# Gate products of one batch in seven block products instead of eight, their block sums on VectorE, and a new order of work for the last graph

## The chip, the cores and the metric

The kernel runs on one core of a Trainium2 chip. The core has five engines that run beside each other and wait for each other through semaphores: TensorE (PE, matrix products into the eight banks of PSUM), VectorE (DVE), ScalarE (ACT), GpSimd (POOL) and SyncE (SP, which here only issues DMA). The metric is the device time of one execution in microseconds; lower is better.

## What is computed

64 graphs of 256 nodes with 256 features each pass through two layers. Cut to what matters:

```python
# layer 0, per graph (d = 256)
h = relu(bn1(conv1x1(x)));  h = bn2(conv17(h));  x_conv = relu(h + x)     # conv branch
s = x @ w_se.T + b_se;  A = exp(-dist(s)) * adj
x_nmp = A @ relu(x @ w_msg.T + b_msg)
x_in = concatenate([x_conv, x_nmp])                # 512 features
gi = x_in @ w_ih.T + b_ih                          # 768 columns: r, z, n
gh = x @ w_hh.T + b_hh                             # 768 columns: r, z, n
r = sigmoid(gi_r + gh_r);  z = sigmoid(gi_z + gh_z)
nn = tanh(gi_n + r * gh_n)
x = layernorm(x + (1 - z) * nn + z * x)
# layer 1
h = layernorm(x);  y = relu(adj @ (h @ W_rel) + b_rel + h @ W_root)
out = layernorm(x + y)
```

All of it is float32.

## The kernel before

Everything is written in a fixed order: `manual_schedule` takes each engine's instructions in the order in which the Python code emits them, so the order of calls in the main loop is the order of each queue. PSUM banks come from one pool of eight.

The graphs go in eight batches of eight. The conv branch of a whole batch is one generator, `conv(b)`; it works in the large tile XF (slots V, U, S and S2 of 256 columns each, and HP behind them) with most of its arithmetic on VectorE, and is advanced by `pump()` in small pieces between the steps of the graphs of batch b - 1. While the last batch's graphs run, no batch is left to be convolved, and XF holds nothing that is needed any more.

Graphs are pipelined. In the loop over k (lines 1044 to 1085) one pass does, in this order on PE: the gates of graph k for node half 0 (`gates_rz`, `gates_n`), the transposes of graph k - 1 (`transposes_h`), `gates_rz` for half 1, `passing(k + 1)`, `factors(k + 2)`, `gates_n` for half 1, `project(k - 1)`, `distances(k + 2)`, `messages(k + 3)` and `aggregate(k - 1)`. On VectorE the same pass runs `update(k)` (nn, w, their statistics, h), the evacuation of messages, the mask of k + 2 and the y of k - 1. The last graph, 63, has its own function, `last_graph`, in which each node half is handled by itself.

A gate product has three left operands, each of 256 features by 256 nodes: the transposed x (XT), the message result (NMP) and the conv result (XC). The right operands are w_hh and the two halves of w_ih. For one node half `gates_rz` multiplies six blocks of 128 features by 512 columns (r and z together) into one bank, and `gates_n` does six matmuls of 256 columns into another, since the hidden n part must be kept apart from the input n part:

```python
nc.tensor.matmul(prz, t, wih[:, i, 0:2 * D], start=False, stop=(i == 3))
nc.vector.tensor_add(rz[:, n, :], prz, brzn[:, :2 * D])
nc.scalar.activation(rz[:, n, :], rz[:, n, :], AF.Tanh, scale=0.5)
```

Then `update` (line 733) makes nn from them with two operations of 512 columns on VectorE and a tanh on ScalarE, w with three more, their mean and variance (`stats`), the powers of the variance on GpSimd, and h with two operations that wait for GpSimd. The transposes of the next pass wait for h. `project` copies its two results hr to SBUF on ScalarE, and `aggregate` adds onto the second half of the same banks.

In `last_graph` (line 826) half 0 and half 1 of graph 63 pass through nn, w, h (line 862), `turn_half` (transposes), `project_half` and a last aggregation (line 906), between which the remaining work of graph 62 is placed. Each half of the output is scaled on ScalarE (line 917) with a shift made on GpSimd, and stored by its own DMA.

Of the kernel before, what the change touches and what calls it, by code (L numbers as in the profile page):

```python
# [51 lines left out]
NM = 3 * len(LEAVES) + 2  # L52
SR, ROWS = 32, 36
OB = 7


def tap_matrix():
# [18 lines left out]
def gnn_two_layers(  # L76
# [22 lines left out]
    def bank(name):  # L99
        return psum.tile([P, 512], F32, tag="ps", name=name)  # L100
# [281 lines left out]
    def product(ps, slot, w, m):  # L382
        for c in range(C):
            nc.tensor.matmul(ps, X[:, slot, c * P:(c + 1) * P], w(m, c), start=(c == 0), stop=(c == C - 1))  # L384
# [49 lines left out]
    def conv(b):  # L434
# [122 lines left out]
        def third(j):  # L557
            stt(sl(V + j, 2, 8), sl(V + j, 2, 8), sv[j], sl(U + j, 2, 8))
            yield cost(2)
# [25 lines left out]
            yield from second(j)  # L585
        for j in range(8):
            yield from third(j)

        def channels(q):
            for o in range(C):  # L590
# [26 lines left out]
    def load(k):  # L617

        if k >= B:
            return  # L620
        load_xt(k)
        load_adj(k)
# [9 lines left out]
    def load_x(k):  # L632
        if k < B:
            XG[k] = work.tile([P, C, D], F32, tag="x", name="x")
            nc.sync.dma_start(out=XG[k], in_=x[k].rearrange("(c p) d -> p c d", p=P))
# [83 lines left out]
    def gates_n(k, n):  # L719
# [5 lines left out]
            nc.tensor.matmul(pn[:, :D], t, wih[:, i, 2 * D:], start=(i == 0), stop=(i == 3))  # L725
        nc.vector.tensor_add(RZ[k][1][:, n, :], pn, brzn[:, 2 * D:])  # L726

    def stats(mv, k, src):
        st = work.tile([P, 6], F32, tag="bst", name="bst", bufs=4)
        nc.vector.bn_stats(st, src)  # L730
        nc.vector.bn_aggr(mv[:, k, :], st)  # L731
# [49 lines left out]
    def project(k):  # L781
        hT = H[k]
        hr = work.tile([P, C, D], F32, tag="hr", name="hr", bufs=1)
        outs = []
        for n in range(C):
            ps = bank("ps_out")
            for c in range(C):
                nc.tensor.matmul(ps, hT[:, c, n * P:(n + 1) * P], wrr[:, c, :], start=(c == 0), stop=(c == C - 1))  # L788
            nc.scalar.copy(hr[:, n, :], ps[:, :D])
            outs.append(ps)  # L790
        OUTS[k] = (hr, outs)
# [29 lines left out]
    def step(g):  # L821
        if g is not None:
            next(g, None)


    def last_graph(y_before, k):
        nn, w, y = (work.tile([P, C, D], F32, tag=t, name=t, bufs=b) for t, b in (("nn", 1), ("w", 1), ("y", 2)))
        H[k] = work.tile([P, C, D], F32, tag="h", name="h", bufs=1)
        X1[k] = work.tile([P, C, D], F32, tag="x1", name="x1", bufs=2)

        hT, hr = (XF[:, i * C * D:(i + 1) * C * D].rearrange("p (c n) -> p c n", c=C) for i in range(2))
        outs = []

        def scales(mv, columns):

            q = work.tile([P, 2], F32, tag="q", name="qh", bufs=4)
            for i, (f, e) in enumerate(columns):
                nc.gpsimd.tensor_scalar(q[:, i:i + 1], mv[:, 1:2], f, e, ALU.mult, ALU.add)
            nc.gpsimd.tensor_tensor(q[:, :len(columns)], q[:, :len(columns)], mhalf[:, :len(columns)], ALU.pow)
            return q  # L840

        def shift(mv, q):
            sh = work.tile([P, 1], F32, tag="sh", name="shh", bufs=4)
            nc.gpsimd.tensor_mul(sh, mv[:, 0:1], q[:, 0:1])
            nc.gpsimd.tensor_scalar(sh, sh, -1.0, None, ALU.mult)
            return sh

        def half(n):
            rz, gn = RZ[k]
            a, c = nn[:, n, :], w[:, n, :]  # L850
            stt(a, rz[:, n, :D], 1.0, gn[:, n, D:], op0=ALU.add, op1=ALU.mult)
            stt(a, a, 0.5, gn[:, n, :D])
            nc.scalar.activation(a, a, AF.Tanh)
            yield
            nc.vector.tensor_sub(c, XG[k][:, n, :], a)
            stt(c, rz[:, n, D:], 3.0, c, op0=ALU.add, op1=ALU.mult)
            stt(c, a, 4.0, c)
            mv = work.tile([P, 1, 2], F32, tag="mv", name="mvh", bufs=4)
            stats(mv, 0, c)
            mv = mv[:, 0, :]  # L860
            q = scales(mv, [(1.0, 4 * EPS), (1 + EPS, 4 * EPS * EPS)])
            nc.vector.tensor_scalar(H[k][:, n, :], c, mv[:, 0:1], q[:, 1:2], ALU.subtract, ALU.mult)
            sh = shift(mv, q)
            yield
            nc.scalar.activation(X1[k][:, n, :], c, AF.Identity, bias=sh, scale=q[:, 0:1])
            yield

        def turn_half(n):
            ps = bank("ps_hT")
            for c in range(C):  # L870
                nc.tensor.transpose(ps[:, c * P:(c + 1) * P], H[k][:, n, c * P:(c + 1) * P], ident)
            for c in range(C):
                nc.scalar.activation(hT[:, c, n * P:(n + 1) * P], ps[:, c * P:(c + 1) * P], AF.Identity,
                                     bias=gb[:, 1, c:c + 1], scale=gb[:, 0, c:c + 1])

        def project_half(n):
            ps = bank("ps_out")
            for c in range(C):
                nc.tensor.matmul(ps, hT[:, c, n * P:(n + 1) * P], wrr[:, c, :], start=(c == 0), stop=(c == C - 1))
            nc.scalar.copy(hr[:, n, :], ps[:, :D])  # L880
            outs.append(ps)

        halves_ = [half(n) for n in range(C)]
        gates_rz(k, 0)
        gates_n(k, 0)
        step(y_before)
        transposes_h(k - 1)
        step(halves_[0])
        gates_rz(k, 1)
        step(halves_[0])  # L890
        step(halves_[0])
        gates_n(k, 1)
        step(halves_[1])
        turn_half(0)
        project(k - 1)
        project_half(0)
        step(halves_[1])
        turn_half(1)
        agg = aggregate(k - 1)
        step(agg)  # L900
        project_half(1)
        step(halves_[1])
        step(agg)
        for m in range(C):
            for n in range(C):
                nc.tensor.matmul(outs[n][:, D:], ADJ[k][:, m, n * P:(n + 1) * P], hr[:, m, :], start=False,
                                 stop=(m == C - 1), skip_group_check=True)
        step(agg)
        for n in range(C):
            o = y[:, n, :]  # L910
            nc.vector.tensor_add(o, outs[n][:, D:], brel)
            stt(o, o, 0.0, X1[k][:, n, :], op0=ALU.max, op1=ALU.add)
            mv = work.tile([P, 1, 2], F32, tag="mv3", name="mvy", bufs=4)
            stats(mv, 0, o)
            q = scales(mv[:, 0, :], [(1.0, EPS / 4)])
            sh = shift(mv[:, 0, :], q)
            nc.scalar.activation(o, o, AF.Identity, bias=sh, scale=q[:, 0:1])
            (nc.sync, nc.scalar)[n].dma_start(out=out[k, n * P:(n + 1) * P, :], in_=o)


# [107 lines left out]

    POINTS = 10
    y_left = None  # L1030
    for b in range(NB):
        coming = conv(b + 1) if b + 1 < NB else iter(())
        done, at, goal = 0.0, 0, BG * POINTS - 6

        def pump():
            nonlocal done, at
            at += 1
            while done < CONV_WEIGHT * at / goal:
                t = next(coming, 1e9)
                if t is None:  # L1040
                    break
                done += t

        for k in range(b * BG, min((b + 1) * BG, B - 1)):
            load(k + 3)
            load_x(k + 1)
            up = update(k)
            agg = None
            gates_rz(k, 0)
            pump()  # L1050
            gates_n(k, 0)
            step(y_left)
            pump()
            if k > 0:
                transposes_h(k - 1)
            pump()
            gates_rz(k, 1)
            pump()
            if k + 1 < B:
                passing(k + 1)  # L1060
            pump()
            if k + 2 < B:
                factors(k + 2)
            gates_n(k, 1)
            pump()
            if k > 0:
                project(k - 1)
            step(up)
            pump()
            if k + 2 < B:  # L1070
                distances(k + 2)
            step(up)
            pump()
            if k + 3 < B:
                messages(k + 3)
            step(up)
            pump()
            if k + 2 < B:
                mask(k + 2)
            if k > 0:  # L1080
                agg = aggregate(k - 1)
            step(agg)
            step(agg)
            pump()
            y_left = agg
        for _ in coming:
            pass
    last_graph(y_left, B - 1)


# [41 lines left out]
```

## Time and profile before

| | us |
|---|---|
| median of 8 runs | 2267.99 |
| lowest, highest | 2265.56, 2270.48 |
| the profiled execution | 2267.9 |
| its span in the profile | 2266.1 |
| a graph of the last batch, gate to gate | 25.60 |
| from the last graph's first gate to the end | 37.6 |

The costliest groups of the gates, from the page (line, engine, operation, output from inputs, shapes, count, then busy time in us and mean ns of one, then the engine's idle time before them):

```profile
L711 PE MATMUL ps_rz<-whh,xT 128*128 128x512 f32 x512 | 240.8, 593 | 0.0
L713 PE MATMUL ps_rz<-wih,nmp 128*128 128x512 f32 x512 | 240.6, 592 | 0.0
L713 PE MATMUL ps_rz<-wih,xc 128*128 128x512 f32 x512 | 240.6, 592 | 0.0
L716 DVE TENSOR_TENSOR rz<-ps_rz,brzn 128x512 f32<-128x512 f32 x128 | 87.0, 680 | 189.5 <-PE ps_rz L713 189.5
...
L723 PE MATMUL ps_n<-whh,xT 128*128 128x256 f32 x512 | 131.6, 379 | 0.0
L725 PE MATMUL ps_n<-wih,xc 128*128 128x256 f32 x512 | 131.4, 379 | 0.0
L725 PE MATMUL ps_n<-wih,nmp 128*128 128x256 f32 x512 | 131.4, 379 | 0.0
```

A matmul of the program has two records. Durations of neighbouring records overlap, so the pace of a row of matmuls is read from the starts.

### The profile page before, as it was taken

What the parts mean: (1) busy time and instruction counts of PE and PEld (TensorE: products, weight loads), DVE (VectorE), ACT (ScalarE), POOL (GpSimd) and SP (SyncE); (2) the same over time, 40 slices, a digit from 0 to 9 for tenths busy, and PEclk for the clock granted to TensorE, in tenths of its full rate; (3) what the DMA queues carried; (4) which work ended last, traced back from release to release, by engine and by line L of the source; (5) the groups of instructions that cost most, each with busy time, mean ns of one, the idle gap of its engine ahead of it and who ended that gap; (6) DMA issues with size and microseconds to landing.
All of it is one profiled execution on the core that took longest, in us unless ns stands there. A gap on an engine that the chain in (4) does not pass through costs nothing.

```text
span 2266.1 us, 24485 instructions
## 1 busy us (share of the span) xinstructions
PE 2219.3 (98%) x8386; PEld 1459.2 (64%) x8386; DVE 1678.3 (74%) x3194; ACT 767.9 (34%) x1588; POOL 470.5 (21%) x935
## 2 busy tenths in 40 slices
PE   8999999999999999999999999999999999999998
PEld 5775666666665666656666566666666666666664
DVE  6976889388882988749886597946889388884444
ACT  6433223432234322443224422243222532233333
POOL 0101212221220221213122121221222122221122
PEclk9999999999999999999999999999999999999999
DMA  5932432314423153232522243231433214421100
GB/s 146 313 105 71 139 107 93 101 44 139 135 75 103 38 170 100 79 103 80 162 80 83 85 130 121 74 112 52 139 106 99 93 48 133 140 75 38 43 28 19
DMA packets 212682, 226.68 MB, mean 100 GB/s; under 512 B 22104, under 2 KB 203855, under 8 KB 212559
## 3 DMA queue, kind: packets, MB, share of 16 engines
q1 hardware_dynamic: 190128, 191.27, 26.7%
q10 hardware_dynamic: 22430, 33.86, 4.3%
q8 instruction: 67, 1.10, 0.2%
q14 instruction: 57, 0.46, 0.1%
HBM read 179.22 MB, written 45.88 MB: 99 GB/s over the span
## 4 chain that ended last, share of the span: by engine, by line
PE 80%; DVE 14%; DMA 2%; issue 2%; POOL 1%; ACT 1%; SPq 0%; ACTq 0%; POOLq 0%; DVEq 0%
PE ps_rz L713 17%; PE ps_k L384 10%; PE ps_rz L711 8%; PE ps_n L725 8%; PE ps_out L788 7%; PE ps_c L465 5%; PE ps_nmp L695 5%; DVE XF L103 4%; PE ps_n L723 4%; PE ps_out L800 4%; PE ps_msg L645 4%; PE ps_w L229 2%; DMA w<-w2m 2%; DVE w L103 1%; DVE bst L730 1%
## 5 line engine op out<-in xcount | busy, mean ns | idle before, releaser
L103 DVE SCALAR_TENSOR_TENSOR XF<-XF 128x512 f32<-128x512 f32 (+2 forms) x800 | 507.4, 664 | 7.4
L752 POOL TENSOR_SCALAR q<-mv 128x2 f32<-128x2 f32 x63 | 31.8, 505 | 1453.1 <-DVE mv L731 1453.1
L384 PE MATMUL ps_k<-w,XF 128*128 128x256 f32 x1316 | 298.3, 382 | 14.6 <-ACT AT L685 11.6
L384 PEld LDWEIGHTS ps_k<-w,XF 128*128 128x128 f32 x1316 | 246.5, 190 | 61.1 <-ACT AT L685 17.2
L726 DVE TENSOR_TENSOR gn<-ps_n,brzn 128x512 f32<-128x512 f32 x128 | 87.9, 687 | 236.7 <-PE ps_n L725 236.7
L717 ACT ACTIVATE rz<-rz 128x512 f32<-128x512 f32 x128 | 80.6, 630 | 509.1 <-DVE rz L716 509.1
L711 PE MATMUL ps_rz<-whh,xT 128*128 128x512 f32 x512 | 240.8, 593 | 0.0
L713 PE MATMUL ps_rz<-wih,nmp 128*128 128x512 f32 x512 | 240.6, 592 | 0.0
L713 PE MATMUL ps_rz<-wih,xc 128*128 128x512 f32 x512 | 240.6, 592 | 0.0
L716 DVE TENSOR_TENSOR rz<-ps_rz,brzn 128x512 f32<-128x512 f32 x128 | 87.0, 680 | 189.5 <-PE ps_rz L713 189.5
L788 PE MATMUL ps_out<-wrr,hT 128*128 128x512 f32 x504 | 226.6, 592 | 0.0
L713 PEld LDWEIGHTS ps_rz<-wih,xc 128*128 128x128 f32 x512 | 97.3, 190 | 122.5 <-issue 122.2
L713 PEld LDWEIGHTS ps_rz<-wih,nmp 128*128 128x128 f32 x512 | 97.3, 190 | 122.5 <-issue 122.5
L788 PEld LDWEIGHTS ps_out<-wrr,hT 128*128 128x128 f32 x504 | 95.7, 190 | 96.2 <-issue 86.1
L656 ACT ACTIVATE msg<-msg 128x512 f32<-128x512 f32 x61 | 38.4, 630 | 331.4 <-DVE msg L654 331.4
L645 PE MATMUL ps_msg<-wms,xT 128*128 128x260 f32 x512 | 132.1, 395 | 4.8 <-DVE XF L400 4.8
L711 PEld LDWEIGHTS ps_rz<-whh,xT 128*128 128x128 f32 x512 | 92.2, 190 | 64.8 <-issue 61.2
L723 PE MATMUL ps_n<-whh,xT 128*128 128x256 f32 x512 | 131.6, 379 | 0.0
L725 PE MATMUL ps_n<-wih,xc 128*128 128x256 f32 x512 | 131.4, 379 | 0.0
L725 PE MATMUL ps_n<-wih,nmp 128*128 128x256 f32 x512 | 131.4, 379 | 0.0
L361 DVE TENSOR_TENSOR XF<-XF 128x512 f32<-128x512 f32 (+3 forms) x128 | 126.1, 1010 | 1.7
L465 PE MATMUL ps_c<-xTc,w 128*128 128x512 f32 x256 | 117.8, 603 | 7.3 <-ACT xTc L457 7.3
(139 smaller groups left out, 3498.3 us busy)
## 6 DMA issues: line engine op xcount, KB each, us to landing
w<-w2m SPq DMA_DIRECT2D x105, 768.0 KB, 5.8
xn<-in_x_dram SPq DMA_DIRECT2D x32, 512.0 KB, 4.4
xt<-xTc ACTq DMA_DIRECT2D x32, 512.0 KB, 3.3
xT<-xt SPq DMA_DIRECT2D x64, 256.0 KB, 3.0
xb<-in_x_dram SPq DMA_DIRECT2D x32, 512.0 KB, 6.1
adj<-in_adjT_dram SPq DMA_DIRECT2D x64, 256.0 KB, 2.8
x<-in_x_dram SPq DMA_DIRECT2D x64, 256.0 KB, 3.0
out_dram<-y ACTq DMA_DIRECT2D x63, 256.0 KB, 2.2
```

The source lines that it names most:

```text
L103: nc.vector.scalar_tensor_tensor(o, in0, s, in1, op0=op0, op1=op1)
L361: (nc.vector.tensor_add if add else nc.vector.tensor_sub)(sl(o, n), sl(a, n), sl(b, n))
L384: nc.tensor.matmul(ps, X[:, slot, c * P:(c + 1) * P], w(m, c), start=(c == 0), stop=(c == C - 1))
L465: nc.tensor.matmul(pss[o], w1[:, c, o * P:(o + 1) * P], xTc[:, c, :], start=(c == 0), stop=(c == C - 1))
L645: nc.tensor.matmul(ps[:, :D + 4], XT[k][:, c, m * P:(m + 1) * P], wms[:, c, :], start=(c == 0), stop=(c == C - 1 and not idle))
L695: nc.tensor.matmul(ps[:, d * N:(d + 1) * N], MSG[k][:, m, d * P:(d + 1) * P], AT[k][:, m, :], start=(m == 0), stop=(m == C - 1))
L711: nc.tensor.matmul(prz, XT[k][:, c, q], whh[:, c, 0:2 * D], start=(c == 0), stop=False)
L713: nc.tensor.matmul(prz, t, wih[:, i, 0:2 * D], start=False, stop=(i == 3))
L723: nc.tensor.matmul(pn[:, D:], XT[k][:, c, q], whh[:, c, 2 * D:], start=(c == 0), stop=(c == C - 1))
L725: nc.tensor.matmul(pn[:, :D], t, wih[:, i, 2 * D:], start=(i == 0), stop=(i == 3))
L788: nc.tensor.matmul(ps, hT[:, c, n * P:(n + 1) * P], wrr[:, c, :], start=(c == 0), stop=(c == C - 1))
L800: nc.tensor.matmul(po, ADJ[k][:, m, n * P:(n + 1) * P], hr[:, m, :], start=False, stop=(m == C - 1), skip_group_check=True)
```

## The change

For the first seven graphs of the last batch (56 to 62) the gates are made by `block_gates`. The left operands are seen as 2 x 2 blocks (two node halves by two feature halves), the weights as 2 x 2 blocks (two feature halves by two column halves of each gate). Seven products of sums of blocks, in Winograd's arrangement of Strassen's method, take the place of eight products of blocks. One product covers all three left operands, adding up in one bank: one matmul of 256 columns for x (r and z) and two of 384 for NMP and XC (r, z, n). The hidden n part stays as four plain matmuls of 256 columns. Three pairs of products share a bank: product 5 adds onto product 0's bank, product 2 onto 4's, product 3 onto 6's, each after VectorE has read the first. The results are put together in nine additions of 384 columns on VectorE, in the U region of XF, with two buffers that alternate.

The sums of the left blocks (`block_sums`, four operations of 128 columns for each of three operands) are made one graph ahead, in XF's S region. The sums of the weight blocks (`weight_blocks`) are made once, in the tiles of the filters, while batch 6's graphs run and the conv of the last batch is in its last stages; the sums of graph 56 follow there as soon as its operands exist.

The pass over these graphs has its own loop. In `last_graph` the order is changed: half 1's nn comes before half 0's h, `project(62)` before half 0's transposes, the first part of `aggregate(62)` before half 1's transposes, and the two half projects stand behind both. The second half of the output is scaled by VectorE.

```diff
+HG = 3 * P
...
+        STAGE[b] = "out"
...
+    def weight_blocks():
+        g_ = [work.tile([P, 3, C, D], F32, tag="w2", name="wsum", bufs=3) for _ in range(3)]
...
+        t1, t2, t4, t7 = (made(i) for i in range(4))
+        b11, b12, b21, b22 = plain(0, 0), plain(0, 1), plain(1, 0), plain(1, 1)
+        RIGHT[0] = [b11, b21, b22, t4, t1, t2, t7]
+        for o, a, b in ((t1, b12, b11), (t7, b22, b12), (t2, b22, t1), (t4, b21, t2)):
+            for i in range(2):
+                nc.vector.tensor_sub(o[i], a[i], b[i])
+                yield
+
+    def block_sums(k, i):
...
+        nc.vector.tensor_add(s1, a21, a22)
+        nc.vector.tensor_sub(s2, s1, a11)
+        nc.vector.tensor_sub(s3, a11, a21)
+        nc.vector.tensor_sub(s4, a12, s2)
+        LEFT[k, i] = (a11, a12, s4, a22, s1, s2, s3)
+
+    def block_gates(k):
...
+        def product(ps, i, start):
+            w, wx = RIGHT[0][i]
+            pv = ps[:, :HG].rearrange("p (g e) -> p g e", g=3)
+            for j, (o, left, right) in enumerate(((pv[:, :2], LEFT[k, 0][i], wx), (pv, LEFT[k, 1][i], w[:, 1]),
+                                                  (pv, LEFT[k, 2][i], w[:, 0]))):
+                nc.tensor.matmul(o, left, right, start=start and j == 0, stop=j == 2, skip_group_check=True)
+            return pv
+
+        def onto(n, h, a, b=None):
+            o = blk[:, n, :, h, :]
+            nc.vector.tensor_add(o, a, o if b is None else bias[:, :, b, :])
...
+        a, d = bank("ps_a"), bank("ps_d")
+        onto(0, 0, product(a, 0, True), 0)
+        onto(0, 0, product(d, 1, True))
+        yield
+        b_, c_ = bank("ps_b"), bank("ps_c")
+        onto(1, 1, product(b_, 4, True), 1)
+        onto(1, 1, product(c_, 6, True))
+        yield
+        t = product(a, 5, False)
+        onto(0, 1, t, 1)
+        onto(1, 0, t, 0)
+        onto(0, 1, product(b_, 2, False))
+        squash(0)
+        onto(1, 1, t)
+        onto(1, 0, product(c_, 3, False))
+        squash(1)
+        yield
+        ps = bank("ps_n")
+        for n in range(C):
+            for c in range(C):
+                nc.tensor.matmul(ps[:, n * D:(n + 1) * D], XT[k][:, c, n * P:(n + 1) * P], whh[:, c, 2 * D:],
+                                 start=(c == 0), stop=(c == C - 1))
+        nc.vector.tensor_add(G[:, :, 3 * D:], ps.rearrange("p (n d) -> p n d", n=C),
+                             brzn[:, 3 * D:].unsqueeze(1).to_broadcast([P, C, D]))
...
@@ last_graph, half @@
             q = scales(mv, [(1.0, 4 * EPS), (1 + EPS, 4 * EPS * EPS)])
+            yield
             nc.vector.tensor_scalar(H[k][:, n, :], c, mv[:, 0:1], q[:, 1:2], ALU.subtract, ALU.mult)
@@ last_graph @@
         step(halves_[0])
-        step(halves_[0])
         gates_n(k, 1)
         step(halves_[1])
+        step(halves_[0])
+        step(halves_[0])
+        project(k - 1)
+        step(halves_[1])
         turn_half(0)
-        project(k - 1)
-        project_half(0)
         step(halves_[1])
-        turn_half(1)
         agg = aggregate(k - 1)
         step(agg)
+        turn_half(1)
+        step(halves_[1])
+        project_half(0)
         project_half(1)
-        step(halves_[1])
         step(agg)
...
-            sh = shift(mv[:, 0, :], q)
-            nc.scalar.activation(o, o, AF.Identity, bias=sh, scale=q[:, 0:1])
+            if n == 0:
+                sh = shift(mv[:, 0, :], q)
+                nc.scalar.activation(o, o, AF.Identity, bias=sh, scale=q[:, 0:1])
+            else:
+                nc.vector.tensor_scalar(o, o, mv[:, 0, 0:1], q[:, 0:1], ALU.subtract, ALU.mult)
@@ pump @@
+            if STAGE.get(NB - 1) in ("inverse", "out"):
+                next(sums_left, None)
+            if STAGE.get(NB - 1) == "out" and (NB - 1) * BG in NMP and len(early_sums) > (done < 1e8):
+                block_sums((NB - 1) * BG, early_sums.pop(0))
@@ loop over the last batch @@
+    for k in range(first_k, B - 1):
+        load(k + 3)
+        load_x(k + 1)
+        ga, up = block_gates(k), update(k)
+        step(ga)
+        step(y_left)
+        step(ga)
+        transposes_h(k - 1)
+        step(ga)
+        passing(k + 1)
+        if k + 2 < B:
+            factors(k + 2)
+        step(ga)
+        if k + 2 < B:
+            block_sums(k + 1, 0)
+            block_sums(k + 1, 2)
+        project(k - 1)
+        step(up)
+        if k + 2 < B:
+            distances(k + 2)
+        step(up)
+        if k + 2 < B:
+            block_sums(k + 1, 1)
+        if k + 3 < B:
+            messages(k + 3)
+        step(up)
+        if k + 2 < B:
+            mask(k + 2)
+        agg = aggregate(k - 1)
+        step(agg)
+        step(agg)
+        y_left = agg
```

In the prediction, P0 to P6 are the products by their index in `product`, in the order of emission P0, P1, P4, P6, P5, P2, P3.

More of the change, by code (lines that the diff above doesn't have):

```diff
@@ L726, in gates_n, with plain, made @@
         nc.vector.tensor_add(RZ[k][1][:, n, :], pn, brzn[:, 2 * D:])
+    LEFT, RIGHT = {}, {}
+    def weight_blocks():
+        g_ = [work.tile([P, 3, C, D], F32, tag="w2", name="wsum", bufs=3) for _ in range(3)]
+        g_ = [t.rearrange("p m c o -> p (m c o)") for t in g_]
+        ih = wih.rearrange("p (s c) (g h e) -> p c s g h e", c=C, g=3, h=2)
+        hh = whh[:, :, :2 * D].rearrange("p c (g h e) -> p c g h e", g=2, h=2)
+        def plain(c, h):
+            return ih[:, c, :, :, h, :], hh[:, c, :, h, :]
+        def made(i):
+            o = (i % 2) * 2 * HG
+            return (g_[i // 2][:, o:o + 2 * HG].rearrange("p (s g e) -> p s g e", s=2, g=3),
+                    g_[2][:, i * 2 * P:(i + 1) * 2 * P].rearrange("p (g e) -> p g e", g=2))
+        t1, t2, t4, t7 = (made(i) for i in range(4))
[5 more added lines that the diff above has]
+                yield
@@ new lines, in block_sums @@
+    def block_sums(k, i):
+        if i == 2:
+            xc, g = XC[k]
+            v = xc[:, :, g, :]
+        else:
+            v = (XT, NMP)[i][k]
+        a11, a12, a21, a22 = (v[:, c, n * P:(n + 1) * P] for n in range(C) for c in range(C))
+        at = S * D + ((k % 2) * 3 + i) * 4 * P
+        s1, s2, s3, s4 = (XF[:, at + j * P:at + (j + 1) * P] for j in range(4))
+        nc.vector.tensor_add(s1, a21, a22)
[3 more added lines that the diff above has]
+        LEFT[k, i] = (a11, a12, s4, a22, s1, s2, s3)
@@ new lines, in block_gates, with squash @@
+    def block_gates(k):
+        G = XF[:, U * D + (k % 2) * 8 * D:U * D + (k % 2 + 1) * 8 * D].rearrange("p (n e) -> p n e", n=C)
+        RZ[k] = (G[:, :, :2 * D], G[:, :, 2 * D:])
+        blk = G[:, :, :3 * D].rearrange("p n (g h e) -> p n g h e", g=3, h=2)
+        bias = brzn[:, :3 * D].rearrange("p (g h e) -> p g h e", g=3, h=2)
+        def product(ps, i, start):
[8 more added lines that the diff above has]
+            nc.vector.tensor_add(o, a, o if b is None else bias[:, :, b, :])
+        def squash(n):
+            nc.scalar.activation(G[:, n, :2 * D], G[:, n, :2 * D], AF.Tanh, scale=0.5)
+        a, d = bank("ps_a"), bank("ps_d")
[23 more added lines that the diff above has]
+        yield
@@ L861, in half @@
             q = scales(mv, [(1.0, 4 * EPS), (1 + EPS, 4 * EPS * EPS)])
+            yield
             nc.vector.tensor_scalar(H[k][:, n, :], c, mv[:, 0:1], q[:, 1:2], ALU.subtract, ALU.mult)
@@ L915, in last_graph @@
             q = scales(mv[:, 0, :], [(1.0, EPS / 4)])
-            sh = shift(mv[:, 0, :], q)
-            nc.scalar.activation(o, o, AF.Identity, bias=sh, scale=q[:, 0:1])
+            if n == 0:
+                sh = shift(mv[:, 0, :], q)
+                nc.scalar.activation(o, o, AF.Identity, bias=sh, scale=q[:, 0:1])
+            else:
+                nc.vector.tensor_scalar(o, o, mv[:, 0, 0:1], q[:, 0:1], ALU.subtract, ALU.mult)
             (nc.sync, nc.scalar)[n].dma_start(out=out[k, n * P:(n + 1) * P, :], in_=o)
@@ L1030, in gnn_two_layers @@
     y_left = None
+    sums_left = weight_blocks()
+    early_sums = [0, 1, 2]
     for b in range(NB):
@@ L1042, in pump @@
                 done += t
+            if STAGE.get(NB - 1) in ("inverse", "out"):
+                next(sums_left, None)
+            if STAGE.get(NB - 1) == "out" and (NB - 1) * BG in NMP and len(early_sums) > (done < 1e8):
+                block_sums((NB - 1) * BG, early_sums.pop(0))
+        if b == NB - 1:
+            break
         for k in range(b * BG, min((b + 1) * BG, B - 1)):
@@ L1087, in gnn_two_layers @@
             pass
+    for _ in sums_left:
+        pass
+    first_k = (NB - 1) * BG
+    for i in early_sums:
+        block_sums(first_k, i)
+    for k in range(first_k, B - 1):
[30 more added lines that the diff above has]
+        y_left = agg
     last_graph(y_left, B - 1)
```

## The prediction

> **What bounds the kernel now.** I read the page first (which engine is full), then the stretches of the last batch, then the order of time inside one of its graphs, then the end. From the page, the span, busy times and slices:
>
> ```profile
> span 2266.1 us, 24485 instructions
> PE 2219.3 (98%) x8386; PEld 1459.2 (64%) x8386; DVE 1678.3 (74%) x3194; ACT 767.9 (34%) x1588; POOL 470.5 (21%) x935
> ...
> PE   8999999999999999999999999999999999999998
> ...
> DVE  6976889388882988749886597946889388884444
> ```
>
> TensorE (PE) is full; VectorE (DVE) falls to four tenths in the last 220 us, where no next batch has to be convolved. Stretches of time; columns are length, then busy time of PE, weight loads, DVE, ACT, POOL:
>
> ```profile
> 2130.30:2155.90 25.60, 25.60 (x91) 15.92 (x90) 11.79 (x27) 8.39 (x17) 5.14 (x14) 1.00 0.13 42
> ...
> 2228.50:2266.10 37.60, 27.49 (x89) 15.50 (x87) 19.65 (x50) 11.46 (x24) 10.34 (x31) 0.97 0.06 21
> ```
>
> One graph of the last batch is 25.60 us of unbroken PE work beside 11.79 us of DVE, so PE work taken out there shortens the span until something else is late. Only the last graph's stretch has holes: 37.60 - 27.49 = 10.1 us. The timeline of one graph (start, length, engine):
>
> ```profile
> 2130.32 1.88 PE L711 MATMUL ps_rz<-whh,xT 128*128 128x512 f32 x4
> ...
> 2135.47 1.03 PE L723 MATMUL ps_n<-whh,xT 128*128 128x256 f32 x4
> ...
> 2138.06 0.60 PE L775 MATMUL ps_hT<-ident,h 128*128 128x128 f32 x4
> ...
> 2148.19 3.60 PE L788 MATMUL ps_out<-wrr,hT 128*128 128x512 f32 x8
> ...
> 2152.09 0.63 ACT L739 ACTIVATE nn<-nn 128x512 f32<-128x512 f32 x1
> ...
> 2157.80 0.73 DVE L762 TENSOR_SCALAR h<-w,mv,q 128x256 f32<-128x256 f32 x2 [0.92 <-POOL q L754]
> ...
> 2161.65 0.66 DVE L716 TENSOR_TENSOR rz<-ps_rz,brzn 128x512 f32<-128x512 f32 x1
> ```
>
> Each float32 matmul is two records. Starts give the pace, which the overlapping durations of 592 and 379 ns don't: 12 records of 512 columns from 2130.32 to 2135.47 are 0.429 us each, 12 of 256 up to 2138.06 are 0.216.
>
> **What the Trainium skill says.** "VectorE: DVE Perf Modes", section on the errata, prices a float32 two-tensor operation at (N+151)/0.96 ns. The trace agrees: 0.69 us at 512 and 0.41 to 0.42 at 256. From it I estimate 0.29 us at 128 columns, 0.56 at 384, 0.96 at 768. In the trace an operation that needs its predecessor starts 0.03 us after it ends, an independent one about 0.08 before. "PSUM — Partial Sum Buffer", section on bank collisions, says to guard PSUM by bank; so a matmul that adds onto a bank must wait until DVE has read it. The trace has no such rewrite in the gates. "Advanced Engine Details and Errata", section Memory Cachelines, puts the cost of strided reads on elements that don't share a line; no matmul of the gates before reads its moving operand in pieces.
>
> **The change, part by part.**
>
> *Gate matmuls, seven graphs.* Removed per graph: 24 records of 512 and 24 of 256, 24 x 0.429 + 24 x 0.216 = 15.48 us. Added: seven products, each one matmul of 256 columns and two of 384. A 384-column record, between the two paces, is 0.322; a product is 2 x 0.216 + 4 x 0.322 = 1.72, seven are 12.05. The n part of the hidden state remains, 8 x 0.216 = 1.73. New sum 13.78, saved 1.70 a graph, 11.9 us over seven. PE was unbroken there, so it is all on the path.
>
> *DVE work per graph.* Out: four additions of 512 (2.75 us). In: twelve sums of 128 (0.29 each), nine additions of 384 (0.56), one of 512, together 9.2. DVE goes from 11.8 to about 18 us of a graph of 23.9: not the bound, but its order matters. Call T the start of project (L788) and t = 0 the first product. In the new PE order products P0, P1, P4, P6 take t = 0 to 6.89, the transposes 0.44, and at t = 7.33 P5 adds onto P0's bank. It must wait for DVE's reading of P0, which is queued behind everything of the graph before. Before, the DVE operation in that place (L716) starts at 2161.65, T + 13.46. New in front of it: eight sums behind the gn addition (four take 0.32 + 3 x 0.21 = 0.95, so 1.9 us), which move the end of the nn operations from T + 2.41 to T + 4.31. ACT's tanh started at T + 3.90 anyway, behind the second hr copy, so 1.45 of these are hidden and 0.45 remain. Then four sums of nmp, 0.95 us, in front of h; h idled 0.92 for POOL, which hides all but 0.03. The reading of P0 starts at T + 13.94 and ends at T + 14.50. From project to the next graph is 7.74 us (2148.19 to 2155.93), so it ends at t = 6.76: 0.57 us to spare. No stall in graphs 56 to 61. Before graph 62 there is no message work, and project to the next graph is 5.98 us (2199.41 to 2205.39) while h still waits for POOL: the reading ends at about 14.47 - 5.98 = t 8.49, and P5 waits 1.16 us. Cost 1.2 us, once. Behind P5 on PE stands all the rest. Other waits clear: P4's nmp sum is there by t = 1.0 against 3.9, P2's bank is read by 8.4 against 9.05.
>
> *Weight sums and first sums.* Eight subtractions (four of 768, four of 256) in batch 6's DVE queue: about 4.9 us, less 0.7 of idle time, so 4.2 late near 2018. The first addition of x to the convolution ends then at 2022.0, and its transposes start on PE at 2022.66; the distance banks are released by ACT at about 2025.15, needed at 2025.27. Cost 0, range 0 to 0.5. The sums of graph 56 fit where DVE waits for tanh in graph 55: 0. No DMA is added, and SP's queue keeps its order.
>
> *The end.* The lines that carry it:
>
> ```profile
> 2246.01 0.41 DVE L862 TENSOR_SCALAR h<-w,mvh,qh 128x256 f32<-128x256 f32 x1 [1.36 <-POOL qh L839]
> ...
> 2246.57 0.41 PE L871 MATMUL ps_hT<-ident,h 128*128 128x128 f32 x2 [1.99 <-DVE h L862]
> ...
> 2251.89 0.41 DVE L862 TENSOR_SCALAR h<-w,mvh,qh 128x256 f32<-128x256 f32 x1 [1.37 <-POOL qh L839]
> ...
> 2262.64 0.60 ACT L917 ACTIVATE y<-y,shh,qh 128x256 f32<-128x256 f32 x1 [0.94 <-POOL shh L845]
> 2263.26 0.35 ACTq L918 DMA_DIRECT2D out_dram<-y  x1
> ```
>
> PE waited 1.99 us for the first half's h; now project(62) fills that. Project(62) brings its two copies of hr (0.37 each) along on ACT, ahead of the first half's hT copies; ACT has idle time there, and both land before the aggregation that reads them. The second half's nn goes ahead of the first half's h on DVE: it starts at 2245.39 rather than 2247.13, so the second h comes at about 2250.15 (3.40 us after its w, as in the trace), its transposes at 2250.71, both half projects 3.44 us later are done, and the last aggregation starts at 2254.4 on the old scale instead of 2256.14: 1.74 gained. The second half of the output is scaled by DVE straight after POOL's power (2262.02 + 0.03 + 0.41) instead of through shift and ACT, which ended at 2263.24: 0.75. Together 2.5.
>
> *Sum.* 11.9 + 2.5 - 1.2 = 13.2 us. The profiled execution took 2267.9 (span 2266.1 and 1.8 around it); its sum gives 2254.7. The median of the runs shown, 2267.99, is 0.1 above it, which I leave out.
>
> **Rivals.**
> - *The bank wait bites in every graph.* The spare 0.57 us is small. If DVE's chain is 1.5 us longer than summed (sums at 128 columns or additions in pieces dearer), six graphs lose 0.93 and graph 62 1.5 more: gain 13.2 - 7.1 = 6.1, 2261.8. For it: all twelve sums are short operations that I priced, not saw. Against: most of the chain is measured. Chance 0.15.
> - *Only the matmuls pay.* The end doesn't shorten and batch 6 stalls by 0.5: 2254.7 + 2.5 + 0.5 = 2257.7. For it: many engines take turns there. Chance 0.13.
> - *Slower: moving operands in pieces.* P0, P1 and P2 read plain weights as runs of 128 columns with gaps. Below, 0, since a run of 128 floats fills its lines; above, the skill's page gives no factor, so I take twice the time: 3 x 1.72 x 7 = 36.1 us more, 2290.8. The change loses from 37% longer reads on (13.2/36.1). I take 0. Chance 0.07.
> - *DVE takes over.* 18 of 23.9 us leave no room for it on average; only 0.05 for a result near 2266, by whatever mixture of waits.
>
> **How the numbers follow.** Forecast 2254.7, chance 0.60. Below, no stall in graph 62 and a somewhat shorter end give 2252; above, the second rival and most of the first lie inside 2261.8. Range 2251.8 to 2261.8, which leaves out the slow rival, the mixture and part of the first. A difference within 0.2% (4.5 us) can't be told from none: above 2263.5 it counts as the same. Faster 0.60 + 0.13 + 0.14 = 0.87; same 0.06; slower 0.07.
>
> **What would show it.** Products at 1.72 us each by their starts, P0 like P5: else the strided rival. A graph period of 23.9 us with P5's bank wait absent in graphs 56 to 61 and near 1.2 in graph 62: else the first rival. L604's transposes unmoved. The last aggregation about 1.7 us earlier against the last graph's first gate. Wrong altogether if PE has holes inside the new graphs that total over 1 us each.

## The result, and the profile after

| | before | after |
|---|---|---|
| median, us | 2268.47 (2264.71 to 2271.78, 28 runs) | 2255.86 (2251.39 to 2261.16, 10 runs) |
| ratio, 95% interval | | 0.9946, 0.9938 to 0.9954 |
| the profiled execution | 2267.9 | 2259.01 |
| its span | 2266.1 | 2257.2 |
| one graph of the last batch | 25.61 | 23.91 |
| from the last graph's first gate to the end | 37.60 | 35.28 |

The kernel is faster by 12.6 us at the median; 2254.7 was forecast and 2255.86 measured. The first lines of the page after, which answer to those of before:

```profile
span 2257.2 us, 24641 instructions
PE 2211.0 (98%) x8400; PEld 1463.7 (65%) x8400; DVE 1720.4 (76%) x3329; ACT 767.8 (34%) x1587; POOL 468.1 (21%) x933
...
DVE  6976889478892988739987498865979478896675
```

PE is still full. The low end of DVE's row, where four tenths stood, now reads five to seven. The busy times of one graph (length, then PE, weight loads, DVE, ACT, POOL, granted clock, DMA share, GB/s) say the same:

```profile
2127.70:2151.60 23.90, 23.90 (x94) 16.30 (x93) 17.04 (x46) 8.50 (x17) 5.26 (x14) 1.00 0.14 45
```

23.90 us of unbroken PE work instead of 25.60, beside 17.0 us of DVE instead of 11.8: the trade that the change makes. In the timeline of that graph (start, length, engine, and in brackets an idle time of the engine just before), the products P0 (bank ps_a), P1 (ps_d), P4 (ps_b), P6 (ps_c) and P5 (ps_a again), with DVE's reading of P0 (L791) between them, are:

```profile
2129.41 0.59 PE L786 MATMUL ps_a<-whh,xT 128*128 128x256 f32 x2
2129.85 0.81 PE L786 MATMUL ps_a<-wih,nmp 128*128 128x384 f32 x2
2130.49 0.81 PE L786 MATMUL ps_a<-wih,xc 128*128 128x384 f32 x2
...
2131.14 0.59 PE L786 MATMUL ps_d<-whh,xT 128*128 128x256 f32 x2
...
2132.86 1.89 PE L786 MATMUL ps_b<-wsum,XF 128*128 128x256 f32 x6
...
2134.58 1.89 PE L786 MATMUL ps_c<-wsum,XF 128*128 128x256 f32 x6
...
2135.47 0.53 DVE L791 TENSOR_TENSOR XF<-ps_a,brzn 128x384 f32<-128x384 f32 x1
...
2136.30 0.60 PE L869 MATMUL ps_hT<-ident,h 128*128 128x128 f32 x4
...
2136.74 1.89 PE L786 MATMUL ps_a<-wsum,XF 128*128 128x256 f32 x6
```

Read from starts, P0 lasts 2131.14 - 2129.41 = 1.73 us and P4 2134.58 - 2132.86 = 1.72. P0 reads its weights (whh, wih) in runs of 128 columns with gaps, P4 reads packed sums (wsum): no difference. DVE's reading of P0's bank ends at 2136.00, 6.59 us after the first product; P5, which adds onto that bank, starts at t = 7.33 with no bracket, so no wait.

Where the time went is read best in four stretches, each from one PE instruction to another that both kernels have. The first begins with the last row of 20 records of filter products in batch 6, at 1976.60 us before and 1980.06 after:

| stretch, us | before | after | difference | forecast |
|---|---|---|---|---|
| batch 6's last filter products to graph 56's first gate | 76.90 | 77.64 | +0.74 | 0 |
| graphs 56 to 61 | 151.90 | 141.69 | -10.21 | -10.2 |
| graph 62 | 23.10 | 22.56 | -0.54 | -1.70 + 1.16 |
| the last graph to the end | 37.60 | 35.28 | -2.32 | -2.5 |
| sum | 289.50 | 277.17 | -12.33 | -13.2 |

The spans of the two profiled executions differ by 8.9 us only, because this execution of the kernel after was already 3.5 us later when the first stretch began. No changed instruction runs before that point; the first weight subtraction starts at 1993.28.

The two losses can be seen in the view of PE's waits, after (line waited on, engine and line that released it, us in total, times, longest). Neither of the first two lines below is there before; the third belongs to the end, where PE waited 2.3 us for h before (2.0 and 0.3) and waits 0.6 now:

```profile
PE ps_a L786 <- DVE XF L791: 0.9, 1, 0.9
...
PE ps_dist L685 <- ACT lr L676: 0.7, 1, 0.7
PE ps_hT L966 <- DVE h L957: 0.6, 1, 0.6
```

The first is P5's wait for P0's bank, once, in graph 62:

```profile
2207.18 0.53 DVE L791 TENSOR_TENSOR XF<-ps_a,brzn 128x384 f32<-128x384 f32 x1
2207.76 1.99 PE L786 MATMUL ps_a<-wsum,XF 128*128 128x256 f32 x6 [0.89 <-DVE XF L791]
```

The second is the one that the forecast lacked. Timeline of batch 6, after:

```profile
2021.78 0.68 DVE L718 TENSOR_TENSOR rz<-ps_rz,brzn 128x512 f32<-128x512 f32 x1
...
2022.50 0.63 ACT L719 ACTIVATE rz<-rz 128x512 f32<-128x512 f32 x1 [2.71 <-DVE rz L718]
...
2023.03 0.57 ACT L699 COPY nmp<-ps_nmp 128x512 f32<-128x512 f32 x1
2023.50 0.56 ACT L675 ACTIVATE lr<-ps_sT,lone 36x256 f32<-36x256 f32 x1
2023.96 0.36 ACT L676 COPY lr<-ps_sT 36x256 f32<-36x256 f32 x1
...
2024.37 0.70 PE L685 MATMUL ps_dist<-lr 4*128 4x256 f32 x4 [0.67 <-ACT lr L676]
```

The eight weight subtractions stand in DVE's queue ahead of graph 54's addition of r and z (L718). ACT idles 2.71 us for it, since its next instruction is the tanh of that sum; the copies of lr, which need nothing from DVE, stand behind the tanh; and PE's distance products need lr. The same chain in the kernel before had room to spare, as its timeline shows: lr ended at 2016.70, and the distance products started at 2020.17, without a wait.

```profile
2014.16 0.68 DVE L716 TENSOR_TENSOR rz<-ps_rz,brzn 128x512 f32<-128x512 f32 x1
...
2014.88 0.63 ACT L717 ACTIVATE rz<-rz 128x512 f32<-128x512 f32 x1 [1.55 <-DVE rz L716]
...
2016.34 0.36 ACT L674 COPY lr<-ps_sT 36x256 f32<-36x256 f32 x1
...
2020.17 0.70 PE L683 MATMUL ps_dist<-lr 4*128 4x256 f32 x4
```

### The profile page after: what moved, and what is told of

Same layout as the page of the kernel before. It is cut to its first block, busy times and chain, and to the rows that moved or that the text cites. A ratio compares the mean times of both kernels' runs of the same rounds, so it can differ in the third digit from the quotient of the medians.

```text
span 2257.2 us, 24641 instructions
## 1 busy us (share of the span) xinstructions
PE 2211.0 (98%) x8400; PEld 1463.7 (65%) x8400; DVE 1720.4 (76%) x3329; ACT 767.8 (34%) x1587; POOL 468.1 (21%) x933
## 4 chain that ended last, share of the span: by engine, by line
PE 73%; DVE 19%; DMA 3%; issue 2%; POOL 2%; ACT 1%; SPq 0%; ACTq 0%; POOLq 0%; DVEq 0%
PE ps_rz L715 13%; PE ps_k L385 11%; PE ps_rz L713 7%; PE ps_n L727 6%; DVE XF L104 6%; PE ps_out L882 6%; PE ps_c L466 5%; PE ps_nmp L697 4%; PE ps_msg L647 3%; PE ps_out L894 3%; PE ps_n L725 3%; DMA w<-w2m 3%; PE ps_w L230 2%; DVE w L104 2%; DVE bst L824 1%
## 5 line engine op out<-in xcount | busy, mean ns | idle before, releaser
L728 DVE TENSOR_TENSOR gn<-ps_n,brzn 128x512 f32<-128x512 f32 x114 | 78.2, 686 | 198.4 <-PE ps_n L727 198.4
L713 PE MATMUL ps_rz<-whh,xT 128*128 128x512 f32 x456 | 215.5, 595 | 0.0
L715 PE MATMUL ps_rz<-wih,nmp 128*128 128x512 f32 x456 | 214.3, 592 | 0.0
L715 PE MATMUL ps_rz<-wih,xc 128*128 128x512 f32 x456 | 214.3, 592 | 0.0
L718 DVE TENSOR_TENSOR rz<-ps_rz,brzn 128x512 f32<-128x512 f32 x114 | 77.6, 681 | 156.8 <-PE ps_rz L715 156.7
L715 PEld LDWEIGHTS ps_rz<-wih,xc 128*128 128x128 f32 x456 | 86.6, 190 | 109.1 <-issue 108.8
L715 PEld LDWEIGHTS ps_rz<-wih,nmp 128*128 128x128 f32 x456 | 86.6, 190 | 109.1 <-issue 109.1
L697 PE MATMUL ps_nmp<-AT,msg 128*128 128x256 f32 x512 | 121.1, 379 | 0.0
L713 PEld LDWEIGHTS ps_rz<-whh,xT 128*128 128x128 f32 x456 | 82.6, 191 | 58.3 <-issue 55.1
L894 PE MATMUL ps_out<-hr,adj 128*128 128x256 f32 x504 | 119.5, 380 | 0.0
L883 ACT COPY hr<-ps_out 128x256 f32<-128x256 f32 x126 | 46.8, 372 | 213.8 <-PE ps_out L882 213.8
```

The costliest lines, as they stand in the source:

```text
L697: nc.tensor.matmul(ps[:, d * N:(d + 1) * N], MSG[k][:, m, d * P:(d + 1) * P], AT[k][:, m, :], start=(m == 0), stop=(m == C - 1))
L713: nc.tensor.matmul(prz, XT[k][:, c, q], whh[:, c, 0:2 * D], start=(c == 0), stop=False)
L894: nc.tensor.matmul(po, ADJ[k][:, m, n * P:(n + 1) * P], hr[:, m, :], start=False, stop=(m == C - 1), skip_group_check=True)
```

## The experiments

All but one are edits of the kernel after, and their ratios are against the kernel before. The kernel after itself was run twice more, once in each group where small differences were asked for.

**The kernel after again.**

> The changed kernel itself, beside the others of this group. The four stretches from batch 6's last filter products (to graph 56's first gate matmul; graphs 56 to 62; graph 62; the last graph to the end) should be 77.6, 141.7, 22.6 and 35.3 us again in any execution. If the 10 us between its fastest and slowest execution come from the part ahead of the changed code, as I take it, these four stay within 0.3 us while the span differs; if the new code is unsteady, they differ too.

Measured: 2258.11 us, ratio 0.996 (0.9947 to 0.9972). The four stretches are 77.71, 141.69, 22.57 and 35.29 us, within 0.07 of the first time. In these executions, what moves lies ahead of the stretches.

**Weight sums later.** They begin only with graph 55's steps.

```diff
-            if STAGE.get(NB - 1) in ("inverse", "out"):
+            if STAGE.get(NB - 1) in ("inverse", "out") and k >= (NB - 1) * BG - 1:
                 next(sums_left, None)
```

> The changed kernel with the weight sums from graph 55 on, and nothing else. Theory (the sums delayed VectorE in graph 54, and with it ScalarE's first-in-first-out queue ahead of the distance products): the first stretch falls from 77.6 to 76.9 us. Rival (a wait of the distance products that has nothing to do with the sums): 77.6 stays.

Measured: 2252.99 us, ratio 0.9925 (0.9904 to 0.9947). The first stretch is 76.90 us, the value of before to the last digit, and the wait on lr is gone from the waits. So the 0.74 us belong to the place of the weight sums, and nothing else of the change shows a cost there. The median, however, lay 2.9 to 5.1 us under the two medians of the kernel after so far, and not 0.7, so the run was repeated beside the kernel after.

> The changed kernel once more, as the yardstick of the two kernels beside it. Theory A (the weight sums in batch 6 cost 0.7 us and nothing else; what the medians differ by beyond that comes from the earlier part of the program and is not tied to the kernel): this run falls somewhere in 2251 to 2261. Theory B (the placement of the weight sums is worth 5 us): 2256 to 2260 again.

> The weight sums put off to the last graphs of batch 6, a second time. Theory A: 0.7 us below after_2 within some 3 us of spread, and in the trace 76.9 us from batch 6's last filter products to graph 56's first gate, as the first time. Theory B: about 5 us below after_2, so 2252 to 2254.

Measured: 2256.30 us (ratio 0.9932 to 0.9958) for the kernel after and 2256.37 (0.9932 to 0.9959) with the edit, no difference, and 76.90 us in the stretch again. That is theory A and not B: the edit is worth 0.7 us in the trace, and medians of four or five runs, which for this one kernel lie 3.4 us apart, can't show so little.

**Graph 60's y behind the gates' reads.** In graph 62's pass the last five DVE operations of graph 60's y (the sum with x and the statistics) go behind DVE's readings of P0, P1, P4 and P6. Graph 60 is the one that the pass of graph 61 aggregates; the expectations call this y graph 62's or 61's.

```diff
-        step(y_left)
+        if k < B - 2:
+            step(y_left)
         step(ga)
+        if k == B - 2:
+            step(y_left)
         transposes_h(k - 1)
+        if k == B - 2:
+            step(y_left)
...
         agg = aggregate(k - 1)
         step(agg)
-        step(agg)
+        if k != B - 3:
+            step(agg)
```

> The changed kernel with graph 62's y statistics behind its first four product readings, and nothing else. Theory: P5's wait in graph 62 goes, 22.6 becomes 21.4 us, other stretches unchanged, 1.15 us faster. Rival: P2 or P3 is late next behind the moved statistics, and under 0.5 us remain.

Measured: 2254.96 us, ratio 0.9937 (0.9917 to 0.9957). Graph 62 takes 21.40 us instead of 22.56, and P5's wait is absent from the waits. So the wait cost 1.16 us, and 23.10 - 21.40 = 1.70 is then what the products save in graph 62, as in the six before it.

**Both edits together.**

> The changed kernel with two waits taken away: the weight sums are made only from graph 55 on, and graph 62's y statistics stand behind its first four product readings on VectorE. Theory (two single waits, 0.7 us for the distance products in batch 6 and 1.15 us for P5 in graph 62): first stretch 76.9 instead of 77.6, graph 62 21.4 instead of 22.6, graphs 56 to 62 unchanged at 141.7, the whole 1.85 us faster than the changed kernel. Rival (these waits hide others that are as late): under 0.5 us faster.

> Both waits removed (weight sums put off, graph 61's y behind the gates' reads), a second time. Theory A: 1.9 us below after_2 within some 3 us of spread. Theory B: about 6 us below after_2. Both: below late_weights_2 by 1.2 us, if the spread lets that be seen.

Measured: 2251.35 us (ratio 0.992 to 0.9945) and 2251.45 (0.991 to 0.9937). Timeline of graph 62 in the first of the two:

```profile
2200.08 0.55 DVE L791 TENSOR_TENSOR XF<-ps_a,brzn 128x384 f32<-128x384 f32 x1
...
2201.52 1.89 PE L786 MATMUL ps_a<-wsum,XF 128*128 128x256 f32 x6
```

The reading now ends 0.89 us before P5, which starts without a wait. Both stretches, 76.90 and 21.40, show their gains side by side: 1.9 us in all. Of the versions tried this has the lowest median, 6.8 and 4.9 us under the kernel after in the same groups. The stretches account for 1.9 of it. The rest isn't explained. It lies ahead of the changed instructions: the two profiled executions of this kernel reached the first stretch at 1975.6 and 1974.5 us, the three of the kernel after at 1980.1, 1979.1 and 1973.8. Since one of those three came earlier than both, the traces don't show that the lower start belongs to this kernel.

**The old order of the last graph.** `last_graph` as before, all else as after.

```diff
-            yield
             nc.vector.tensor_scalar(H[k][:, n, :], c, mv[:, 0:1], q[:, 1:2], ALU.subtract, ALU.mult)
...
-            if n == 0:
-                sh = shift(mv[:, 0, :], q)
-                nc.scalar.activation(o, o, AF.Identity, bias=sh, scale=q[:, 0:1])
-            else:
-                nc.vector.tensor_scalar(o, o, mv[:, 0, 0:1], q[:, 0:1], ALU.subtract, ALU.mult)
+            sh = shift(mv[:, 0, :], q)
+            nc.scalar.activation(o, o, AF.Identity, bias=sh, scale=q[:, 0:1])
```

(and the steps between the halves in their old order)

> The changed kernel with the last graph in the order and with the output scaling of the kernel before. Theory: the last stretch goes back from 35.3 to 37.6 us, 2.3 us slower than the changed kernel, the other stretches unchanged. Rival (graph 62's later finish had already moved the end, and the new order is worth little): under 1 us slower.

Measured: 2257.4 us, ratio 0.9958 (0.9945 to 0.997). The last stretch is 37.58 us, as before, and the others are unchanged. The end is worth 2.29 us. This kernel has the block gates with the old end, so the rest of the gain is theirs.

**No sums of the left blocks** for graphs 57 to 62.

```diff
+            if k == (NB - 1) * BG:
+                nc.vector.tensor_add(s1, a21, a22)
...
```

> The changed kernel without the block sums of graphs 57 to 62: the sum operations on VectorE are left out, and the products read whatever their places hold. Theory (PE sets the pace, the sums lie beside it): graphs 56 to 62 stay at 141.7 us, graph 62 loses 0.45 us of its wait (22.1), in all 0.4 to 0.5 us faster. Rival (VectorE's 2.8 us of sums per graph are partly on the path): 1 us or more per graph, 6 us or more in all.

Measured: 2256.77 us, ratio 0.9955 (0.9942 to 0.9969). The graphs keep 23.91 us. The reading of P0 ends 6.25 us after the first product instead of 6.59, and graph 62 takes 22.24 us instead of 22.57. So twelve sums, 2.85 us of DVE time by the prediction's figures, push the reading by 0.34 us. DVE's waits hide the rest: without the sums it idles 2.15 us for the tanh before w and 0.92 us for POOL before h, with them 0.69 and nothing. The 72 fewer operations gain nothing outside graph 62.

**The same sums made twice.**

```diff
+        for _ in range(1 if k == (NB - 1) * BG else 2):
+            nc.vector.tensor_add(s1, a21, a22)
...
```

> The changed kernel with every block sum of graphs 57 to 62 made twice, 2.8 us more on VectorE per graph. Theory (P5 waits until VectorE has read P0, with 0.74 us to spare): eight more sums move nn by 1.86 us, four more move h by another 0.8, so P0 is read 2.65 us later and P5 waits 1.9 us in each of graphs 57 to 61 and about 1.9 us longer in graph 62: 141.7 becomes 151.3, graph 62 24.5, in all 11 to 12 us slower, no gain left. Rival (VectorE has 6 us to spare per graph, so 2.8 more are hidden): unchanged.

Measured: 2268.14 us, ratio 0.9995 (0.9983 to 1.0008): the whole gain is gone, as was expected. Graph 56, whose own sums aren't doubled, keeps 23.91 us; graphs 57 to 61 take 2.0 us more each, and graph 62 takes 24.44, 1.9 more, part of which is a wait of P4 for its doubled nmp sums (1.1 us). In its waits:

```profile
PE ps_a L787 <- DVE XF L792: 10.1, 6, 1.8
```

and in the timeline of one graph, whose first product started at 2129.59:

```profile
2138.24 0.53 DVE L792 TENSOR_TENSOR XF<-ps_a,brzn 128x384 f32<-128x384 f32 x1
...
2138.82 1.99 PE L787 MATMUL ps_a<-wsum,XF 128*128 128x256 f32 x6 [1.75 <-DVE XF L792]
```

The first twelve sums cost the reading 0.34 us, the second twelve 2.59 (it ends at t = 9.18 instead of 6.59). The idle times that hid the first twelve are used up (before w it stays at 0.69 us, before h there is none), and 2.59 less the 0.74 us to spare is 1.85, nearly all of the 2.0 lost. This is the first rival's mechanism made to happen: it is real, and the change stays 0.74 us short of it.

**Spare DVE work in the other batches.** The kernel before, with twelve additions of 128 columns and nine of 256 in each of graphs 1 to 55 and constants as operands, at the places where the block sums and additions would stand. It asks whether block gates could pay in the other batches too.

```diff
+    extra = work.tile([P, 2 * P], F32, name="extra", bufs=1)
+    def spare(n, w):
+        if 0 < k < (NB - 1) * BG:
+            for _ in range(n):
+                nc.vector.tensor_add(extra[:, :w], brzn[:, :w], brzn[:, 2 * P:2 * P + w])
...
             gates_rz(k, 0)
+            spare(3, 2 * P)
```

(and six of 256 after `gates_rz` for half 1, eight of 128 ahead of `project`, four ahead of `messages`)

> The kernel before with VectorE work like that of the block gates added to every graph of batches 0 to 6 (twelve additions of 128 columns and nine of 256 of a constant, about 5.5 us per graph, used by nobody); the gates themselves are unchanged, the output too. It asks why only the last batch has block gates. Theory: VectorE is 77% busy there, at 97 to 100% in the stretches of the transforms, so the additions land on the path there: 2 to 3 us per graph, 110 to 160 us in all, more than the 1.70 us per graph that block gates would save (94 us over 55 graphs). Rival (7.9 us of idle VectorE time per graph hide it): under 30 us.

Measured: 2495.46 us, ratio 1.0994 (1.0962 to 1.1026): 228 us longer, 4.1 us for each of the 55 graphs, more than the 2 to 3 that were expected and more than the 1.7 that block gates save. The additions took 400.2 us of DVE, 7.3 us a graph, where 5.5 were reckoned; by the prediction's figures the block gates add 9.2 - 2.75 = 6.4, so the test is somewhat too hard. A stretch of 300 us in the middle (PE, weight loads, DVE, ACT, POOL, granted clock), and the longest waits of PE:

```profile
1100.00:1400.00 300.00, 274.63 (x998) 179.32 (x997) 259.65 (x558) 87.32 (x182) 58.20 (x114) 0.97 0.28 90
```

```profile
PE ps_hT L775 <- DVE h L762: 51.6, 15, 5.7
PE ps_k L384 <- ACT AT L685: 46.4, 14, 3.6
PE ps_rz L711 <- ACT AT L685: 14.9, 7, 2.4
```

In the same kind of stretch of the kernel before, DVE had 208 of 271 us. It is now at 260 of 300, so 40 us of it are still free, but not where PE waits. One of the longest waits, in the same columns:

```profile
532.40:537.90 5.50, 0.00 (x0) 0.00 (x0) 5.26 (x17) 0.38 (x1) 3.03 (x7) 0.90 0.19 48
```

PE does nothing, and DVE is busy. Counted over all of PE's waits of more than half a microsecond in these batches, 163 us, DVE is busy for 148. Its free time lies elsewhere, where it waits for gate products (L716 and L726, 299 us in DVE's waits). So an average with room in it hides stretches without any, which is what the expectation said.

PE's idle time grew from 39 to 183 us. Part of the rest isn't waiting at all: in 208 places neighbouring records of the filter products start 0.42 us apart instead of 0.21 (none in the kernel before), 44 us in these products alone, and the granted clock falls to 0.96 over the whole span.

## Why the prediction was right

*Gate matmuls, 11.9 us: right.* The product takes 1.72 us as worked out, the graph 23.91, and 7 x 1.70 is found once the wait in graph 62 is taken away. The strided rival fell at once: P0 and P4 have the same pace. The caution came from the Trainium skill, "Advanced Engine Details and Errata", section Memory Cachelines; the trace agrees with the lower bound that the prediction drew from it: runs of 128 floats with gaps behind them cost nothing here (1.73 us a product against 1.72).

*DVE's chain and the bank wait: right.* The forecast had P0's reading end at t = 6.76 and 0.57 us to spare in graphs 56 to 61; the trace has 6.59 and 0.74. Most of the difference is the sums, priced at 0.48 us of delay and measured at 0.34: the eight in front of nn moved its end to T + 4.08 and not to T + 4.31. In graph 62 it forecast a wait of 1.16 us: removing it gave 1.16 back, and the trace agrees: P5 starts at t = 8.38, 1.05 us late, and runs 0.1 longer. The prices of the sums hold: (N+151)/0.96 ns of "VectorE: DVE Perf Modes", the section on the errata, gives 0.29, 0.56 and 0.96 us for 128, 384 and 768 columns, and the trace shows 0.26 to 0.29, 0.52 to 0.56 and 0.95. What no price tells is how much of a chain is hidden: the first twelve sums cost 0.34 us, the next twelve 2.59.

*Weight sums in batch 6, "Cost 0, range 0 to 0.5": wrong, they cost 0.74.* The lateness was right (4.2 forecast; the addition L718 was 4.16 us late, once the 3.46 us of the whole execution are taken off). The step followed it to the conv's transposes and to the distance banks, and neither waited. It missed the lr copies, which need neither the sums nor the late addition and merely stand behind the tanh in ACT's queue. The sign that the prediction named, transposes that don't move, failed by the same 0.74 us: they follow the distance products on PE. This is the only step whose mechanism failed, and putting the sums off showed it. It is also the half of the second rival that came true; its other half, an end that doesn't shorten, didn't.

*The end, 2.5: 2.3.* The last aggregation came 1.79 us earlier against the last graph's first gate (1.74 forecast), although h still kept the second half's transposes waiting 0.6. The scaling on DVE gave 0.5 instead of 0.75. The lines that tell why, from the timelines of the end, before and then after:

```profile
2256.14 2.19 PE L906 MATMUL ps_out<-XF,adj 128*128 128x256 f32 x8
...
2259.91 0.57 POOL L839 TENSOR_TENSOR qh<-qh,mhalf 128x1 f32<-128x1 f32 x1
...
2261.44 0.58 POOL L839 TENSOR_TENSOR qh<-qh,mhalf 128x1 f32<-128x1 f32 x1
```

```profile
2247.79 2.19 PE L1003 MATMUL ps_out<-XF,adj 128*128 128x256 f32 x8
...
2251.56 0.85 POOL L933 TENSOR_TENSOR qh<-qh,mhalf 128x1 f32<-128x1 f32 x1
...
2253.35 0.58 POOL L933 TENSOR_TENSOR qh<-qh,mhalf 128x1 f32<-128x1 f32 x1
2253.96 0.41 DVE L1017 TENSOR_SCALAR y<-y,mvy,qh 128x256 f32<-128x256 f32 x1 [1.30 <-POOL qh L933]
```

The first half's power took 0.85 us on POOL; before it took 0.57, and it does again with the old end. The second half's power waits behind it in POOL's queue and starts 5.56 us after the last aggregation instead of 5.30, about 0.25 late. The power takes 0.85 us in all ten runs with the new end. POOL had idled longer in front of it (2.96 us against 0.67 before), but the length of the idle time alone doesn't explain it: powers of 128x2 in the same execution took 0.71 us after 2.87 and 3.46 us of idle time, and 0.88 to 1.15 after 2.29 and 2.61. The cause stays open.

*The forecast as a whole.* 12.33 us were found where 13.2 were forecast: 0.74 of the 0.87 between them are the weight sums, the rest is the end. The median measured, 2255.86, is 1.2 us over the forecast. That it came so close has luck in it, since the executions spread by 10 us and two more medians of the same kernel are 2258.11 and 2256.30; the stretches are the better test. The three further kernels that hold one part back or take one wait out move the stretch that they touch and no other, so the parts add up as the sum took them.

## What to carry to other kernels

To trade matrix work for vector work, look for a stretch in which the vector engine has time to spare, and then price the chain and not the total: here twelve small operations cost 0.34 us and twelve more 2.59, with over a quarter of the engine's time idle in the first case. When something is put into an in-order queue, follow the delay through the queues of the engines that wait for it, to work that stands behind the wait and has nothing to do with it. To judge a part worth a microsecond in a kernel whose executions spread by ten, compare the stretch between two instructions that both traces have; the median can't show it.

## What was not expected of the hardware

The executions of the kernel after spread from 2251.4 to 2261.2 us, while its last 277 us repeat within 0.12 in three traces. Two of these traces were laid side by side (the first and the third): they drift apart by 6.3 us before the changed part. Some steps of it follow a wait for a filter's DMA (7 waits, 3.8 us in one; 1 wait, 0.2 in the other). Others are runs of matmuls at half pace, each record 0.42 us instead of 0.21. Such half-paced neighbours among the filter products number 16 in one, 8 in the other, 0 in the kernel before and 208 in the kernel with spare DVE work.

All of them lie where the trace gives PE a granted clock of 0.5. From the first execution of the kernel after (length, then PE, weight loads, DVE, ACT, POOL, granted clock):

```profile
561.50:564.90 3.40, 3.40 (x10) 2.69 (x9) 3.26 (x8) 0.33 (x1) 0.00 (x0) 0.50 0.00 0
564.90:569.00 4.10, 4.10 (x20) 3.58 (x20) 3.12 (x9) 0.00 (x0) 2.27 (x5) 1.00 0.00 0
```

PE had stood idle for 1.1 us just before. Eight records at twice the time make such a spell cost 1.7 us. How often one follows an idle time of PE can be counted in the batches between 220 and 2200 us. With the spare DVE work a spell followed each of the 28 waits of 3 us or more, 2 of the 4 between 2 and 3 us, and 4 of the 24 between 1 and 2 us. In the kernel after it followed 2 of 9 waits between 1 and 2 us in one execution and 1 of 7 in the other, in the kernel before none of 7; longer ones there are none in that part. So in these runs a wait of 3 us was always followed by half pace, and one of 1.1 us, which comes once with each batch's filter products, only at times. What decides in the second case stays open.
